# Token lists from products of ones-and-zeros rows, and a state scaled ahead of its addition

## The chip, the cores and the metric

The kernel runs on one core of a Trainium2 chip. A core has five engines with queues of their own, each strictly in order: TensorE (PE; its weight loads are shown apart as PEld), VectorE (DVE), ScalarE (ACT), GpSimd (POOL) and SyncE (SP), which here only issues transfers. Sixteen DMA engines move data; SP, ACT and POOL can all issue to them. The metric is the device time of one execution in microseconds (us).

## The reference, cut to what matters

Two layers on 4096 tokens (8 batches of 512) of 256 numbers.

```python
def L0_attn(u):        # a state-space layer, run forward and backward, chunks of 128 tokens
    ...
    states = einsum('bcln,bhcl,bclhp->bchpn', B, decay_states, x)
    new_states = einsum('bhzc,bchpn->bzhpn', decay_chunk, states)   # state * decay + addition
    ...
def L0_ffn(x):         # every token goes to its best of 8 experts (256 -> 1024 -> 256)
    p = softmax(x @ Wr + br); e = argmax(p)
    y = p[e] * (relu(x @ W1[e] + b1[e]) @ W2[e] + b2[e])
def L1_attn(x):        # attention, 16 heads, products of queries and keys over 512 tokens
    ...
def L1_ffn(x):         # two best of 8 experts, 512 places each; the last "expert" returns its input
    ...
```

The two expert layers matter here. In each, a program on the chip must turn "token t goes to expert e with weight m" into a list: which token stands at which place of an expert, and its weight. Layer 0 cuts the sorted tokens into 39 blocks of 128 rows (`NBLK`), each of one expert. Layer 1 has 7 experts with 512 places, 28 groups of 128 (`NSLOT1 // P`).

## The kernel before

**Start.** `rows_in` loads the tokens in four pairs of batches. For a pair DVE takes means and variances (L358), ACT normalises into `xn` (L366), PE transposes (L386), ACT copies the transposed tiles out (L387), PE makes the small projection with step sizes and the expert logits (L392), and ACT copies that into `proj` (L396). `xn` holds 272 numbers a row: 256 of the token, its number, its weight, and padding.

**Layer 0's lists.** `route0` makes the softmax, takes the best expert, ranks the tokens of each expert (`ranks`) and computes for each token the row `slot0` of a sorted copy `xd0` in DRAM. 32 indirect transfers from POOL (L473), 128 rows each, scatter the rows of `xn` to it. `xd0` has been filled with blank rows before (L376, number out of range), so that free rows are known. `step_sizes` works out step sizes and decays; `decays` and `edges` follow.

**The expert blocks of layer 0.** `blocks` is a generator: at each `yield` it has recorded one piece. `fetch` asks for the block's rows `xd` (SP, a plain load of 128 rows), and for `w1`, `b12` and `w2` (POOL, indirect by `w_idx`). A block is two halves of 16 PE instructions (L583) with bias and relu on ACT (L590) or DVE (L592), a turn of the next block's rows, and the second product (L604). The result is scaled by the weight that came with the row (`xd[:, DM+1]`) and scattered by the number that came with it to `yt0` (`put`, L559).

**The chunk loop.** 64 chunks (8 batches, 4 steps, 2 directions) are recorded by hand in one order for all engines (`manual_schedule`). For a chunk: `segments`, `cross`, `inside` (L1077), `before` (the old state's share: L1095 on PE, L1096 on DVE, L1097 on POOL), `pairs`, `behind` (the new state: L1103 on PE, the scaling L1109 on POOL, the addition L1112 on DVE). Between them `turn()` places parts of the next and last batch and `fill(1)` advances the generator chain `rows` (route0, then blocks) by a yield; when it has run out, each fill advances `late` instead. Ahead of the loop `send(k)` advances `rows` by k yields; it is used 39 times there in all, and those 39 yields are just route0's.

**The join of the layers.** `late` first loads the weights of the second layer (`second_weights`), then runs three chains in turn: `norm(b)` (read x1, add yt0 to it by a POOL transfer, normalise, write `xn1`), `turn(b)` (transpose, logits, and the projections of the attention), `route(lo, hi)` (ranks and places for a group of batches, for 0 to 4, 4 to 7 and 7 to 8). A batch is taken only when its chunks are done. `route` writes `slot1` and then scatters pairs of number and weight, 8 bytes a row, by 64 indirect transfers from POOL (L758) to `tab` in DRAM, which ACT's queue has cleared (L1256). What `late` has left at the end of the chunk loop is done between the first steps of layer 1's attention.

**Layer 1.** 128 steps of attention; `experts` loads the list `slots` from `tab`, gathers rows of `xn1` by it (L1297) and runs between the steps, paced by `due()`.

A tile of a pool with one buffer, asked for again under the same tag, must wait until all readers of the old one are done.

Of the kernel before, what the change touches and what calls it, by code (L numbers as in the profile page):

```python
# [40 lines left out]
DW = DM + 16  # L41
FAR = NSLOT1 * P
# [18 lines left out]
def tile_kernel(ctx: ExitStack, tc: tile.TileContext, t, out: bass.AP):  # L61
# [36 lines left out]
    blank = ctile("blank", [P, DW])  # L98
    G.memset(blank, 0.0)
    G.iota(blank[:, DM : DM + 1].bitcast(I32), pattern=[[0, 1]], base=NT, channel_multiplier=1)  # L100


    xd0 = dram.tile([NBLK * P, DW], FP, name="xd0", tag="xd0")
    yt0 = dram.tile([NT, DM], FP, name="yt0", tag="yt0")
    tab = dram.tile([NSLOT1, 2], FP, name="tab", tag="tab")
# [13 lines left out]
    def clear(dst, rows, lo, hi):  # L119

        n = rows // P
        A.dma_start(
            out=dst[: n * P, :].rearrange("(p r) d -> p r d", p=P)[:, lo:hi, :],
            in_=bc(blank[:, : dst.shape[1]], 1, [P, hi - lo, dst.shape[1]]),
        )

# [44 lines left out]
    def ranks(pool, bank, mask, hold):  # L171
# [18 lines left out]
        rank = pool.tile(shape, FP, name="rk_r", tag="rk_r")  # L190
        V.tensor_tensor(rank, cum, total, ALU.subtract)
        V.tensor_tensor(rank, rank, pre, ALU.add)
# [4 lines left out]
    def slots_of(pool, oh, where, tag):  # L197

        n = oh.shape[1]
        pick = pool.tile([P, n, NE], FP, name="so_p", tag="so_p")  # L200
        V.tensor_tensor(pick, oh, where, ALU.mult)
        s = pool.tile([P, n], FP, name="so_s" + tag, tag="so_s" + tag)
        V.tensor_reduce(s, pick, AX.X, ALU.add)
        return s

# [58 lines left out]
    def rows_qk():  # L264
# [8 lines left out]
    xs = ctx.enter_context(ExitStack())  # L273
    xn = xs.enter_context(tc.tile_pool(name="x0", bufs=1, side="right")).tile(
        [P, NTILE, DW], FP, name="xn0", tag="xn0"
    )
    G.memset(xn[:, :, DM:], 0.0)
    G.iota(xn[:, :, DM].bitcast(I32), pattern=[[P, NTILE]], base=0, channel_multiplier=1)
# [29 lines left out]
    w_in = ctile("w_in", [P, KC, 2 * P * HC + NXBC * P - DI], pool=l0c)  # L308
# [25 lines left out]
    slot0 = l0c.tile([P, NTILE], I32, name="slot0", tag="slot0")  # L334
# [15 lines left out]
    def rows_in():  # L350

        G2 = 2 * TPB
        for u, b0 in zip(us, order[::2]):
# [10 lines left out]
            V.scalar_tensor_tensor(nm, mv[:, :, 0], -1.0, rs, ALU.mult, ALU.mult)  # L364
            for i in range(G2):
                A.activation(  # L366
                    xn[:, b0 * TPB + i, :DM], u[:, i, :], AF.Identity,
                    bias=nm[:, i : i + 1], scale=rs[:, i : i + 1],
                )
            if b0 == order[0]:  # L370
                Y.dma_start(out=w_in, in_=t["w_in"])
            if b0 == order[2]:
                n = NBLK // B + 1
                for k in range(B):
                    lo, hi = k * n, min(NBLK, (k + 1) * n)
                    Y.dma_start(  # L376
                        out=xd0.rearrange("(p r) d -> p r d", p=P)[:, lo:hi, :],
                        in_=bc(blank, 1, [P, hi - lo, DW]),
                    )
            xTs = {}  # L380
            for b in both:
                xTs[b] = m2.tile([P, KC, S], FP, name="xT", tag="xT")
                for k in range(KC):
                    tp = bank("tp", [P, S], 0)
                    for c in range(TPB):
                        T.transpose(tp[:, c * P : (c + 1) * P], xn[:, b * TPB + c, k * P : (k + 1) * P], ident)  # L386
                    A.copy(xTs[b][:, k, :], tp)  # L387
            for b in both:
# [7 lines left out]
                A.copy(proj[:, b * TPB : (b + 1) * TPB, :], pp)  # L396
                if b > 1:
                    Y.dma_start(out=xtd[b], in_=xTs[b])
        return xTs

    def step_sizes():
# [6 lines left out]
        ea = big.tile([P, 2 * NH], FP, name="ea", tag="ea")  # L408
# [1381 lines left out]
```

## Time and profile before

Three runs took 2043.42, 2045.7 and 2048.68 us; the median is 2045.7.

| | |
|---|---|
| the profiled execution's own time | 2045.05 us |
| its span, first to last instruction | 2043.4 us |
| mean granted PE clock | 0.941 |
| PE busy | 1807.3 us (88%) |
| DVE busy | 1416.6 us (69%) |
| ACT busy | 1180.8 us (58%) |
| POOL busy | 683.8 us (33%) |
| data moved by DMA | 244.56 MB |
| L473, scatters of layer 0's rows | 32, 32.7 us of POOL |
| L758, scatters of layer 1's pairs | 64, 64.7 us of POOL |
| L1109, scaling of the state | 32, 35.5 us of POOL |
| DVE at L1112 waiting for L1109 | 68.2 us, 16 times, longest 11.6 |
| SP's queue at L533 (`xd` loads) waiting for scatters of L559 | 336.1 us, 31 times |

The stages in time: tokens in until 67.6 us; route0 and step sizes until 98.6; the first batch's parts until 153.3, where the first product of the chunk loop (L1077) runs; expert blocks beside the chunks until about 860; the join until the first experts of layer 1 at about 1260; attention and experts to the end. Times in the profile are from the span's start. A bracket at the end of a line of the timeline gives the idle time of that engine ahead of the instruction and what ended it.

### The profile page before, as it was taken

What the parts mean: (1) busy time and instruction counts of PE and PEld (TensorE: products, weight loads), DVE (VectorE), ACT (ScalarE), POOL (GpSimd) and SP (SyncE); (2) the same over time, 40 slices, a digit from 0 to 9 for tenths busy, and PEclk for the clock granted to TensorE, in tenths of its full rate; (3) what the DMA queues carried; (4) which work ended last, traced back from release to release, by engine and by line L of the source; (5) the groups of instructions that cost most, each with busy time, mean ns of one, the idle gap of its engine ahead of it and who ended that gap; (6) DMA issues with size and microseconds to landing.
All of it is one profiled execution on the core that took longest, in us unless ns stands there. A gap on an engine that the chain in (4) does not pass through costs nothing.

```text
span 2043.4 us, 33598 instructions
## 1 busy us (share of the span) xinstructions
PE 1807.3 (88%) x11768; PEld 1226.2 (60%) x11768; DVE 1416.6 (69%) x3296; ACT 1180.8 (58%) x2592; POOL 683.8 (33%) x620
## 2 busy tenths in 40 slices
PE   6458799999999999969878778999999999999997
PEld 5326577776776666635545545666666666666654
DVE  4574575766757585566672658888787878788885
ACT  4233354544544444345443237878788877788886
POOL 0265465654656555342247222111111111111030
PEclk9778899999999999979988768999999999999999
DMA  8035754555555455254532323131313131314171
GB/s 284 25 107 206 148 187 163 184 174 174 195 179 188 141 188 173 80 134 123 155 99 91 96 70 111 45 102 47 101 48 102 39 103 39 101 42 118 37 140 47
DMA packets 145895, 244.56 MB, mean 120 GB/s; under 512 B 26269, under 2 KB 106015, under 8 KB 133824
## 3 DMA queue, kind: packets, MB, share of 16 engines
q1 hardware_dynamic: 108080, 126.56, 20.1%
q0 software_dynamic: 33392, 115.18, 19.1%
q10 hardware_dynamic: 4256, 0.69, 0.4%
q8 instruction: 94, 1.54, 0.3%
q14 instruction: 73, 0.60, 0.1%
HBM read 183.93 MB, written 59.36 MB: 119 GB/s over the span
## 4 chain that ended last, share of the span: by engine, by line
PE 60%; DVE 12%; ACT 12%; issue 5%; DMA 4%; POOL 3%; SPq 0%; POOLq 0%; ACTq 0%; DVEq 0%
PE p_ps L1505 7%; PE y_ps L604 6%; PE pj L852 6%; PE h_ps L583 6%; ACT s L1498 6%; PE o_ps L1514 5%; PE e_hp L1333 4%; PE s_ps L1483 4%; PE e_yp L1346 4%; ACT pT L1506 3%; PE op L996 2%; PE seg L1039 2%; PE yd L1077 2%; PE sp L1103 2%; DVE cv L865 1%
## 5 line engine op out<-in xcount | busy, mean ns | idle before, releaser
L1488 DVE TENSOR_SCALAR s<-s_ps 128x512 f32<-128x512 f32 x512 | 318.1, 684 | 140.3 <-PE s_ps L1483 138.8
L1498 ACT ACTIVATE s<-s,ng 128x512 f32<-128x512 f32 x512 | 330.9, 717 | 23.2 <-DMA kT<-kd 23.2
L1490 DVE CUSTOM_DVE_ANT_0 s<-s,band 128x512 f32<-128x512 f32 x512 | 323.1, 687 | 0.0
L1506 ACT COPY pT<-p_ps 128x512 f32<-128x512 f32 x512 | 275.5, 588 | 61.2 <-PE p_ps L1505 54.3
L1505 PE MATMUL p_ps<-ident,s 128*128 128x128 f32 x2048 | 284.9, 282 | 21.8 <-ACT pT L1506 16.8
L1505 PEld LDWEIGHTS p_ps<-ident,s 128*128 128x128 f32 x2048 | 235.2, 143 | 95.7 <-ACT pT L1506 33.5
L1353 POOL DMA_INDIRECT x<-e_yo,slots x28 | 45.8, 1635 | 622.3 <-ACT e_yo L1352 622.3
L852 PE MATMUL pj<-xT,w_in 128*128 128x512 f32 x384 | 199.4, 645 | 18.0 <-DVE cv L865 10.1
L583 PEld LDWEIGHTS h_ps<-xdT,w 128*128 128x128 f32 x1248 | 151.1, 194 | 24.5 <-issue 23.5
L1483 PE MATMUL s_ps<-kT,qT 16*128 16x512 f32 x1024 | 159.4, 662 | 5.6 <-DMA kT<-kd 4.4
L583 PE MATMUL h_ps<-xdT,w 128*128 128x128 f32 x1248 | 154.8, 278 | 3.5 <-DMA w<-in_w_dram,w_idx 3.5
L865 DVE SCALAR_TENSOR_TENSOR cv<-pj,w_conv_w,cv 128x511 f32<-128x511 f32 (+2 forms) x192 | 143.2, 746 | 12.5 <-ACT cv L861 8.0
L604 PE MATMUL y_ps<-w,hT 128*128 128x256 f32 x624 | 151.1, 386 | 0.0
L1097 POOL TENSOR_TENSOR yT<-yT,ex 128x512 f32<-128x512 f32 (+1 forms) x48 | 59.3, 1235 | 243.7 <-DVE ex L1096 174.9
L604 PEld LDWEIGHTS y_ps<-w,hT 128*128 128x128 f32 x624 | 118.2, 194 | 34.9 <-issue 18.7
L1333 PE MATMUL e_hp<-e_xdT,e_w 128*128 128x256 f32 x448 | 121.6, 394 | 10.1 <-ACT e_hT L1336 9.1
L852 PEld LDWEIGHTS pj<-xT,w_in 128*128 128x128 f32 x384 | 70.2, 201 | 98.7 <-issue 81.7
L1514 PE MATMUL o_ps<-pT,vt 128*32 128x256 f32 x2048 | 127.5, 388 | 0.0
L1077 PE MATMUL yd<-mt,xdt 128*64 128x128 f32 x1024 | 77.1, 297 | 42.6 <-DVE mt L1071 23.4
L1346 PE MATMUL e_yp<-e_w,e_hT 128*128 128x256 f32 x448 | 113.3, 385 | 0.2 <-ACT e_hT L1336 0.2
L1514 PEld LDWEIGHTS o_ps<-pT,vt 128*32 128x32 f32 x2048 | 61.3, 111 | 84.4 <-issue 51.5
L1052 ACT ACTIVATE mt<-seg,mid 64x64 f32<-64x64 f32 x512 | 109.4, 309 | 0.8
(301 smaller groups left out, 3056.9 us busy)
## 6 DMA issues: line engine op xcount, KB each, us to landing
ex<-exd SPq DMA_DIRECT2D x96, 128.0 KB
fr<-fdd SPq DMA_DIRECT2D x64, 128.0 KB
od<-os SPq DMA_DIRECT2D x28, 256.0 KB
e_w<-in_ei_dram SPq DMA_DIRECT2D x7, 1024.0 KB
e_w<-in_eo_dram SPq DMA_DIRECT2D x7, 1024.0 KB
xd<-xd SPq DMA_DIRECT2D x39, 136.0 KB
xd<-blank SPq DMA_DIRECT2D x7, 680.0 KB
vd<-vt SPq DMA_DIRECT2D x16, 288.0 KB
```

The lines of the kernel that those rows point to most:

```text
L583: T.matmul(hp[:, i, :], w1[:, k * FF + f * P : k * FF + (f + 1) * P], xdT[:, k * P : (k + 1) * P], start=(k == 0), stop=(k == KC - 1),)
L604: T.matmul(yp, hT[f // 4][:, f % 4, :], w2[:, f * DM : (f + 1) * DM], start=(f == 0), stop=(f == FC - 1))
L852: T.matmul(pj, w_in[:, k, o * P : (o + 1) * P], self.xT[:, k, :], start=(k == 0), stop=(k == KC - 1))
L1333: T.matmul(hp, w1[:, k, f * P : (f + 1) * P], xdT[:, k, :], start=(k == 0), stop=(k == KC - 1))
L1346: T.matmul(yp, hT[:, f, c * P : (c + 1) * P], w2[:, f, :], start=(f == 0), stop=(f == FC - 1))
L1483: T.matmul(sp[i], self.q[r, cols], self.k[r, :], start=True, stop=True)
L1488: V.tensor_scalar(self.p[i], sp[i], -CLAMP, CLAMP, ALU.max, ALU.min)
L1490: V.tensor_tensor_reduce(out=self.p[i], in0=self.p[i], in1=band[:, at : at + S], scale=1.0, scalar=-3.0e38, op0=ALU.mult, op1=ALU.max, acc ...
L1498: A.activation(self.p[i], self.p[i], AF.Exp, bias=self.ng[:, i : i + 1])
L1505: T.transpose(pp[:, k, :], self.p[i][:, k * P : (k + 1) * P], ident)
L1506: A.copy(pT[i][:, :, cc * P : (cc + 1) * P], pp)
L1514: T.matmul(op[32 * i : 32 * i + 32, half * 2 * P : (half + 1) * 2 * P], self.v[:, k, h * (AD + 1) : h * (AD + 1) + 32], pT[i][:, k, :], st ...
```

## The change

Layer 0: `xn`, its numbers and padding are gone. ACT normalises in place, SP writes the rows to `xn0` in DRAM (8 stores), and the transposes read the same tiles. `proj` and one of two transposed tiles of the first two batches are copied by DVE, the former one pair later. `xd0` and its clears are gone. `route0` splits each place into block and row (`locate`), and `enter` builds, for eight tiles at a time, rows of ones and zeros on DVE and multiplies them on PE, adding up a table of number and weight for each place. `numbers` turns it into integers (a free place gives a number past the last token). The blocks gather their rows by it. `b12` becomes part of `w2`'s rows. `route0` has 8 yields in place of 39; ahead of the loop `rows` is advanced 9 times and then once with each of some 13 slots.

Layer 1: the same in place of `slot1`, `tab` and 64 scatters, two tiles at a time, one group of four entries for each batch and yield; the table stays in SBUF. `route` takes batches 0 to 5 and 5 to 8. `second_weights` yields three times more, `norm` twice more behind its first addition, `w_o` is loaded at the start of layer 1.

The chunk loop: the state's scaling on POOL stands in `before`, ahead of L1097, and not in `behind`. The first product of `start` is POOL's for the first batch. The clear of `tab` is gone, that of `xn1`'s last rows has another form.

```diff
+    def locate(pool, at):
+        n = at.shape[1]
+        i = pool.tile([P, n], I32, name="lc_i", tag="lc_i")
+        V.tensor_copy(i, at)
+        V.tensor_scalar(i, i, 7, None, ALU.logical_shift_right)
+        hi = pool.tile([P, n], FP, name="lc_h", tag="lc_h", bufs=2)
+        V.tensor_copy(hi, i)
+        lo = pool.tile([P, n], FP, name="lc_l", tag="lc_l", bufs=2)
+        V.scalar_tensor_tensor(lo, hi, -float(P), at, ALU.mult, ALU.add)
+        return lo, hi
+
+    def enter(pool, to, lo, hi, pair, first, last):
+        n, blocks = lo.shape[1], to.shape[1]
+        row_of = pool.tile([P, n, P], FP, name="en_r", tag="en_r")
+        V.tensor_tensor(row_of, bc(lo, 2, [P, n, P]), bc(iota_p, 1, [P, n, P]), ALU.is_equal)
+        of = pool.tile([P, n, blocks], FP, name="en_b", tag="en_b")
+        V.tensor_tensor(of, bc(hi, 2, [P, n, blocks]), bc(iota_p[:, :blocks], 1, [P, n, blocks]), ALU.is_equal)
+        what = pool.tile([P, n, blocks, 2], FP, name="en_w", tag="en_w")
+        V.tensor_tensor(what, bc(of, 3, [P, n, blocks, 2]), bc(pair, 2, [P, n, blocks, 2]), ALU.mult)
+        for i in range(n):
+            T.matmul(
+                to.rearrange("p b k -> p (b k)"), row_of[:, i, :], what[:, i].rearrange("p b k -> p (b k)"),
+                start=(first and i == 0), stop=(last and i == n - 1),
+            )
+
+    def numbers(pool, table, to):
+        none = pool.tile([P, table.shape[1]], FP, name="nu_n", tag="nu_n")
+        V.tensor_scalar(none, table[:, :, 0], 0.0, nowhere, ALU.is_equal, ALU.mult)
+        V.scalar_tensor_tensor(to, table[:, :, 0], -1.0, none, ALU.add, ALU.add)
...
-                A.copy(proj[:, b * TPB : (b + 1) * TPB, :], pp)
+                pps.append((b, pp))
...
+        tp = bank("tab", [P, NBLK, 2], "e")
+        n = 2 * TPB
+        for i in range(0, NTILE, n):
+            at = slice(i, i + n)
+            enter(big, tp, lo[:, at], hi[:, at], pair0[:, at, :], i == 0, i + n == NTILE)
+        V.tensor_copy(table0, tp)
+        numbers(big, table0, number0)
...
-                        Y.dma_start(out=w, in_=xd0[j * P : (j + 1) * P, :])
+                        G.indirect_dma_start(
+                            out=w, out_offset=None, in_=xn0, bounds_check=NT + P - 1, oob_is_err=True,
+                            in_offset=bass.IndirectOffsetOnAxis(ap=number0[:, j : j + 1], axis=0),
+                        )
...
-                for i in range(lo * TPB, hi * TPB):
-                    for k in range(2):
-                        one = G.indirect_dma_start(
-                            out=tab, out_offset=bass.IndirectOffsetOnAxis(ap=slot1[:, i, k : k + 1], axis=0),
...
+                    for i in range(0, n, TPB):
+                        yield
+                        tp = late_bank("tab1", [P, NSLOT1 // P, 2])
+                        for h in range(0, TPB, 2):
+                            at = slice(i + h, i + h + 2)
+                            own = slice(lo * TPB + i + h, lo * TPB + i + h + 2)
+                            for k, (row_, block) in enumerate(where):
+                                enter(
+                                    pool, tp, row_[:, at], block[:, at], pairs[:, own, k, :],
+                                    h == 0 and k == 0, h == 2 and k == 1,
+                                )
+                        V.tensor_tensor(slots, slots, tp, ALU.add)
...
+                if not self.last:
+                    G.tensor_tensor(
+                        heads(st), heads(st), bc(dec_all[:, self.d, self.i, :], 2, HP), ALU.mult
+                    )
                 V.tensor_tensor(self.ex, self.ex, yo, ALU.mult)
                 G.tensor_tensor(self.yv, self.yv, self.ex[:, :, self.span], ALU.add)
...
-                    d = self.d
-                    G.tensor_tensor(
-                        heads(st), heads(st), bc(dec_all[:, d, self.i, :], 2, HP), ALU.mult
-                    )
                     V.tensor_tensor(st, st, sp, ALU.add)
```

## The prediction

> **What bounds the kernel now.** I read the busy tenths in 40 slices first, then busy time by stages, then the chain of waits and the timeline at the places where TensorE (PE) is not full.
>
> ```profile
> PE   6458799999999999969878778999999999999997
> DMA  8035754555555455254532323131313131314171
> 75.00:100.00 25.00, 2.48 (x7) 1.85 (x8) 22.55 (x51) 0.00 (x0) 10.68 (x10) 0.54 0.15 51
> 100.00:125.00 25.00, 18.22 (x40) 5.60 (x39) 12.61 (x21) 9.57 (x21) 14.71 (x15) 0.71 0.24 84
> 125.00:150.00 25.00, 14.02 (x35) 5.93 (x33) 21.97 (x28) 9.33 (x19) 15.75 (x15) 0.80 0.42 136
> 250.00:800.00 550.00, 535.24 (x3240) 387.69 (x3239) 369.97 (x631) 260.46 (x731) 315.65 (x273) 0.99 0.54 178
> 860.00:1260.00 400.00, 312.68 (x1563) 190.73 (x1562) 249.04 (x682) 175.86 (x407) 155.90 (x152) 0.82 0.38 110
> ```
>
> The columns of a stage are its limits, its length, then busy time and count of PE, weight loads, DVE, ACT, POOL, then granted clock, DMA share and GB/s. From 250 to 800 us PE is busy 97%: there only PE work counts, and work of other engines is free. Two stages have holes: the start (0 to 250) and the join of the layers (860 to 1260, PE idle 22%). The change works in both. From 1300 on PE is about 95% busy again and nothing is edited, so what the joints win or lose reaches the end.
>
> **The start, part by part.** Up to 67.6 us four pairs of batches run in lockstep, because ACT copies the projection out before it normalises the next pair:
>
> ```profile
> 35.04 0.24 ACT L396 COPY proj<-pp 128x96 f32<-128x96 f32 x1 [2.65 <-PE pp L392]
> 38.46 0.24 ACT L396 COPY proj<-pp 128x96 f32<-128x96 f32 x1 [3.18 <-PE pp L392]
> 31.56 6.86 PE L392 MATMUL pp<-w_w_small,xT 128*128 128x24 f32 x32
> ```
>
> A pair takes 13.4 us (norms begin at 11.88, 25.24, 38.59). With the copy on DVE, ACT normalises under those products; what is left on PE is 6.9 us of products and about 4.2 us of transposes, 11.1. Three pairs save 3 x 2.3 and the last pair's wait for a transposed tile (2.3 us, on the store of xT) shrinks with three buffers: 8 us. Low end 0, should 4 MB of new row stores take the place of the 5.3 MB of clears that are gone; high end 9.
>
> The lists of layer 0 replace 32 scatters, which sat on POOL (about 1.0 us and 0.30 issue each, 86 to 137 us) beside DVE work, so removing them wins nothing there. They add, on the DVE path between slot0 (84.98 us) and the step sizes (85.07): five small operations for row and block, 1.0; four groups of eight tiles. In a group DVE compares 1024 numbers a row (1.23, as L1071 at its best), 312 (0.48, between 0.43 for 256 and 0.69 for 512) and multiplies 624 (0.84): 2.55. Then PE makes 8 products, each two instructions: L392 has the same weights and a short moving side, 6.86/32 = 0.214 us, so 3.4; the later L583 runs 16 in 1.95. The row tile has one buffer, so the next group's compare waits for these products and the two add up, with 0.2 for the hand-overs. 4 x (2.55 + 3.4 + 0.2) = 24.6. Then copy and numbers 0.8, and the block's weight index, which moves ahead of the step sizes, 2.1 (98.73 to 100.98 now). Sum 28.5 late; 22.7 with the fast products. I take 28.5, since PE is as idle there as at L392.
>
> The trace grants PE 0.54 of its clock in 75 to 100 us. The Trainium skill (TensorE: Matmul & The Clock Gate, Part 1: The HAM clock gate) says the clock halves after an idle window of some 3.4 us and is given back after one that is busy. By it four groups with 2.55 us of DVE between them could even keep the clock full, 22.7 by the sum above; the slow row speaks for 28.5.
>
> In exchange 14 pieces of the expert blocks of layer 0, 2.4 blocks, are dealt out ahead of the chunk loop. A block is 8.1 us of PE (4 x 1.95 first halves and products of L604 at 1.89 per 8, and 0.4 transposes). In the loop that is PE time saved: 2.4 x 8.1 = 19.4. Ahead of the loop the pieces lie in a stretch (98.6 to 153.3 us) with 17.8 us of PE idle between 100 and 150; they need 18.6 us at the fast rows and about 30 at the slow ones (16 of L583 took 3.75 at 161 us), and DVE and ACT must wait for them in order. I add 4; ends -3 (PE's clock rises) and +12. The first x by fr product goes to POOL for the first batch: DVE is spared 4 x 0.69, but its neighbours slow down:
>
> ```profile
> 143.85 2.98 DVE L922 SCALAR_TENSOR_TENSOR yT<-x,w_d_rep,yT 128x511 f32<-128x511 f32 x2
> 258.32 1.53 DVE L922 SCALAR_TENSOR_TENSOR yT<-x,w_d_rep,yT 128x511 f32<-128x511 f32 x2
> ```
>
> The first ran beside POOL's products of L938, the second did not. So POOL gives back what DVE wins: 0. The Trainium skill (SBUF — State Buffer, Who interferes with whom) has the rule: a DVE instruction with two inputs in SBUF contends with a GpSimd instruction that reads SBUF, and one blocks fully. It speaks against moving work to POOL; the pair above agrees, 2.98 against 1.53.
>
> Two stalls go. The first expert weights are asked for early and not at 155 us, where the chain of waits has 5.75 us of DMA w<-in_w_dram,w_idx: -5.75 (0 if the gathers come late too). And this one:
>
> ```profile
> 212.04 0.58 ACTq L1256 DMA_DIRECT2D tab<-blank  x1
> 210.00:220.00 10.00, 10.00 (x80) 7.39 (x79) 7.74 (x17) 5.70 (x18) 7.67 (x7) 1.00 0.60 21
> 220.00:230.00 10.00, 10.00 (x54) 6.04 (x53) 2.88 (x4) 2.64 (x4) 6.23 (x7) 1.00 0.90 56
> 244.69 0.69 DVE L915 TENSOR_TENSOR yT<-x,fr 128x512 f32<-128x512 f32 x1 [12.35 <-DMA fr<-fdd]
> ```
>
> The clear of tab goes out in pieces of 8 bytes; the DMA engines are 60 and 90% busy and move 21 and 56 GB/s. A store of 16 KB (fdd) issued at 221.56 is 19.24 us on the chain of waits, and PE idles 11.0 us between 230 and 250. The clear is gone: -11 (low -5, should other transfers hold the store).
>
> Start: -8 + 28.5 + 4 - 19.4 - 5.75 - 11 = **-11.7 us**.
>
> The block fetches: 39 loads of xd leave SP's queue, where they waited 336 us for scatters, and come to POOL as gathers; 39 fetches of b12 leave POOL. A gather is 1.14 (L1297) and a b12 fetch 1.15, so POOL is even. SP's queue is freed, but PE is full beside it: 0.
>
> **The join.** Three more yields after the second weights' loads: PE waited 7.5 us for w_dn: -7.5 (0 to -7.5). Two more after the first read-add: DVE waited 7.3 us for xr<-yt and PE 9.85 behind it: -7 (0 to -9.9). Then POOL:
>
> ```profile
> 1076.21 0.69 DVE L1112 TENSOR_TENSOR st<-st,sp 128x512 f32<-128x512 f32 x1 [5.69 <-POOL st L1109]
> 1093.23 0.69 DVE L1112 TENSOR_TENSOR st<-st,sp 128x512 f32<-128x512 f32 x1 [11.64 <-POOL st L1109]
> 1110.41 0.69 DVE L1112 TENSOR_TENSOR st<-st,sp 128x512 f32<-128x512 f32 x1 [7.62 <-POOL st L1109]
> ```
>
> Chunks come every 17.1 us because POOL holds eight scatters of 1.28 between its products, and the state's scaling stands behind them. The first 32 of the 64 scatters lie here. DVE waits 25 us, PE idles 8.6 in 1060 to 1120: I take -12 between (ends -5 and -20). Scaling ahead of the addition, elsewhere in the join: 5 us of L1112 waits left, -3 (0 to -5). POOL's addition to yT then waits one product of 1.1 us longer; nothing waits for it soon. One pass of route fewer spares some 45 DVE instructions of 0.2: -6 (0 to -9).
>
> Against it stand 8 groups of 4 entries. An entry is 0.92 us of DVE (0.43 for 256 numbers, 0.21 for 56, 0.28 for 112) and 4 PE instructions of 0.117; again one buffer, so DVE and PE take turns. PE loses three turns of 0.92 + 0.15 and 1.9 of its own: 5.1 a group, 41 for eight, less the 22% that PE idles there anyway: +33. Ends: 15 (PE's own work alone) and 56 (turns on both engines, 7.0 a group). Join: -7.5 - 7 - 12 - 3 - 6 + 33 = **-2.5 us**.
>
> Together -14.2. The profiled execution took 2045.05 us (span 2043.4 and 1.65 around it), 0.65 under the median of 2045.7; so **2031 us**, own range 2005 to 2039.
>
> **Rivals.**
> 1. *The turns of the lists decide* (slower). Each small product waits for DVE and each compare for PE; the join has DVE and PE handing over already (PE's waits for DVE add up to over 50 us in 800 to 1260). Entries at 56 (+23) and the start's pieces at +12 (+8): 2031 + 31 = 2062. It decides from 5.9 us a group, where 8 groups eat the -14.2. Against it: DVE runs ahead of PE where PE is full.
> 2. *The early blocks buy idle fills* (no change). Late work is gated by finished batches, so blocks that end earlier may leave empty turns in 860 to 1150 and not time. 14.4 of the 19.4 are lost: 2045.
> 3. *POOL was the whole trouble of the join.* Without scatters the entries hide (+15 for +33) and -20 for -12, -9.9 for -7: 2031 - 29 = 2002.
>
> That it does not do what it says is unlikely: every scatter line is deleted.
>
> **Numbers.** Forecast 0.52, rival 1 0.28, rival 2 0.10, rival 3 0.10. Under 0.3% (6 us) this kernel's measurement can't tell from no change. Faster: nine tenths of the forecast, all of rival 3 and a little of rival 2, 0.60; same 0.12; slower 0.28. Range 1994 to 2068.
>
> **What would show it.** Right: the last projection copy at 58 to 62 us; da at 112 to 119 us (98.6 now); the first yd product at 168 to 180 (153.3) with two blocks done; no PE hole near 240; L1112 waits under 35 us in all (68.2); a list group in the join of 5 us on PE. Wrong: groups of 6 us or more, waits of h_ps for the gathered xd, or a PE idle share in the join that does not fall below 22%.

## The result, and the profile after

Four runs of the kernel after took 2073.52, 2060.61, 2068.46 and 2061.94 us, median 2065.2; the kernel before, beside it, 2044.56. The ratio is 1.0103, 95% interval [1.0063, 1.0143]: 1% slower, where 2031 us was forecast. The profiled execution is the slowest of the four, 2073.52 us (span 2071.8), 28.5 more than that of before (2045.05); the medians differ by 20.6.

The busy tenths of the kernel after, in 40 slices of 51.8 us; the third line is the granted clock in tenths:

```profile
PE   6567999999999999789877867999999999999997
PEclk7589999999999999899967766999999999999999
DMA  7044554554645462445302312131313131314161
```

The same stages as before, then the two places that matter. Columns as in the prediction: limits, length, busy time and count of PE, PEld, DVE, ACT and POOL, granted clock, DMA share, GB/s:

```profile
75.00:100.00 25.00, 14.77 (x64) 13.95 (x64) 9.56 (x13) 0.00 (x0) 0.00 (x0) 0.50 0.00 1
100.00:125.00 25.00, 9.96 (x31) 5.06 (x32) 19.32 (x32) 4.97 (x14) 10.09 (x9) 0.61 0.54 201
125.00:150.00 25.00, 20.09 (x90) 11.77 (x88) 13.85 (x23) 9.43 (x19) 4.64 (x5) 0.93 0.24 84
250.00:800.00 550.00, 535.26 (x3256) 387.08 (x3255) 373.68 (x626) 262.84 (x737) 310.54 (x270) 0.99 0.52 174
860.00:1260.00 400.00, 317.26 (x1522) 197.55 (x1524) 246.15 (x647) 156.05 (x368) 81.34 (x73) 0.80 0.31 92
1040.00:1100.00 60.00, 42.79 (x158) 29.86 (x159) 28.03 (x96) 5.53 (x15) 4.49 (x4) 0.59 0.07 22
1230.00:1270.00 40.00, 19.78 (x94) 13.52 (x92) 23.84 (x84) 4.92 (x9) 0.12 (x1) 0.54 0.02 7
```

PE's fifth slice (207 to 259 us) stands at 9 for 7 before: the hole near 240 is gone (230 to 250 us: 20.00 of 20 busy), and POOL's work in the join is halved (81 for 156 us). But in 1040 to 1100 and 1230 to 1270 no engine is full, PE's clock falls to 0.59 and 0.54, and ACT, POOL and the DMA engines all but stop. Those are the list groups of layer 1: five in the first routing pass, three in the second. The timeline of the kernel after inside one group, DVE and PE:

```profile
1048.72 0.42 DVE L217 TENSOR_TENSOR en_r<-lc_l,iota_p 128x256 f32<-128x256 f32 x1 [3.98 <-PE tab L223]
1049.06 0.21 DVE L219 TENSOR_TENSOR en_b<-lc_h,iota_p 128x56 f32<-128x56 f32 x1
1049.31 0.28 DVE L221 TENSOR_TENSOR en_w<-en_b,pairs 128x112 f32<-128x112 f32 x1
1049.64 1.10 PE L223 MATMUL tab<-en_w,en_r 128*128 128x56 f32 x4 [0.95 <-DVE en_w L221]
1050.78 0.42 DVE L217 TENSOR_TENSOR en_r<-lc_l,iota_p 128x256 f32<-128x256 f32 x1 [1.20 <-PE tab L223]
...
1051.69 1.10 PE L223 MATMUL tab<-en_w,en_r 128*128 128x56 f32 x4 [0.95 <-DVE en_w L221]
...
1053.75 1.10 PE L223 MATMUL tab<-en_w,en_r 128*128 128x56 f32 x4 [0.95 <-DVE en_w L221]
```

An entry comes every 2.05 us: PE works 1.10 and waits 0.95 for DVE, DVE waits 1.20 for PE. Four such entries are 8.2 us, and all that is queued behind them on both engines waits too. Over the eight groups, PE is busy 32.8 us with the 128 instructions and waits 37.0 us for their rows, 69.8 together (busy time, mean ns of one, then the waits and what ended them):

```profile
L223 PE MATMUL tab<-en_w,en_r 128*128 128x56 f32 x128 | 32.8, 406 | 37.5 <-DVE en_w L221 37.0 <-ACT lat L246 0.5
```

The lines of the start that answer to those of before, from the timeline of the kernel after: the last projection copies, on DVE now, a pair of the first batch's scaled additions (L960), the first `yd`, and the second batch's first product with `fr`:

```profile
52.90 0.26 DVE L383 COPY proj<-pp 128x96 f32<-128x96 f32 x1 [2.55 <-PE pp L420]
56.31 0.26 DVE L383 COPY proj<-pp 128x96 f32<-128x96 f32 x1 [3.16 <-PE pp L420]
...
157.28 1.79 DVE L960 SCALAR_TENSOR_TENSOR yT<-x,w_d_rep,yT 128x511 f32<-128x511 f32 x2
...
178.69 1.98 PE L1115 MATMUL yd<-mt,xdt 128*64 128x128 f32 x16 [7.45 <-DVE mt L1109]
...
252.04 0.68 DVE L953 TENSOR_TENSOR yT<-x,fr 128x512 f32<-128x512 f32 x1
```

The tokens are in at 56.31 us for 67.6, DVE no longer waits 12.35 us for `fr`, and the scaled additions of the first batch took 1.79 a pair at most, where the slow pair before took 2.98; the first `yd` is 25.4 us later, inside the recorded 168 to 180.

Where the 28.5 us come from, by the starts of `yd` products (chunks counted from 0) and of layer 1's score products (`s_ps`) in the two profiled executions:

| place | before | after | after − before |
|---|---|---|---|
| chunk 0 | 153.30 | 178.69 | +25.4 |
| chunk 16 | 403.86 | 409.22 | +5.4 |
| chunk 40 | 763.08 | 769.36 | +6.3 |
| chunk 57 | 1053.00 | 1027.28 | −25.7 |
| chunk 59 | 1078.09 | 1106.60 | +28.5 |
| chunk 63 | 1138.90 | 1144.54 | +5.6 |
| first score step | 1175.27 | 1173.91 | −1.4 |
| seventh score step | 1240.83 | 1274.64 | +33.8 |
| own time | 2045.05 | 2073.52 | +28.5 |

The kernel after was 26 us ahead at chunk 57. The first pass's groups cost it 54 us in two chunks. Part of that comes back, as before pays there for its scatters (chunks of 17.1 us), and the second pass's groups take 35 again. These are two single executions: two more of after had the first `yd` at 174.65 and 178.90 and chunk 40 at 764.42 and 770.31.

### The profile page after: what moved, and what is told of

Same layout as the page of the kernel before. It is cut to its first block, busy times and chain, and to the rows that moved or that the text cites. A ratio compares the mean times of both kernels' runs of the same rounds, so it can differ in the third digit from the quotient of the medians.

```text
span 2071.8 us, 33710 instructions
## 1 busy us (share of the span) xinstructions
PE 1839.1 (89%) x11956; PEld 1256.2 (61%) x11956; DVE 1461.9 (71%) x3374; ACT 1178.4 (57%) x2581; POOL 585.2 (28%) x528
## 3 DMA queue, kind: packets, MB, share of 16 engines
q10 hardware_dynamic: 1040, 0.66, 0.1%
## 4 chain that ended last, share of the span: by engine, by line
PE 39%; ACT 11%; DVE 9%; issue 1%; DMA 1%; SPq 0%; ACTq 0%; DVEq 0%; POOLq 0%
PE p_ps L1540 8%; ACT s L1533 6%; PE o_ps L1549 5%; PE e_hp L1368 4%; PE s_ps L1518 4%; PE e_yp L1381 4%; ACT pT L1541 3%; PE tab L223 2%; PE op L1034 2%; DVE s L1525 1%; PE pj L889 1%; DVE s L1523 1%; PE qp L258 1%; PE yd L1115 1%; PE fin L1481 1%
## 5 line engine op out<-in xcount | busy, mean ns | idle before, releaser
L1388 POOL DMA_INDIRECT x<-e_yo,number x28 | 45.7, 1633 | 629.1 <-ACT e_yo L1387 622.9
L889 PE MATMUL pj<-xT,w_w_in 128*128 128x512 f32 x384 | 197.1, 638 | 6.2 <-DVE z L995 4.0
L637 PEld LDWEIGHTS y_ps<-w,hT 128*128 128x128 f32 x624 | 118.3, 195 | 34.9 <-issue 17.1
L1368 PE MATMUL e_hp<-e_xdT,e_w 128*128 128x256 f32 x448 | 121.5, 394 | 11.2 <-ACT e_hT L1371 9.1
L889 PEld LDWEIGHTS pj<-xT,w_w_in 128*128 128x128 f32 x384 | 70.1, 200 | 85.3 <-issue 73.5
L1061 POOL TENSOR_TENSOR au<-da,half 128x512 f32<-128x512 f32 x64 | 77.7, 1215 | 149.4 <-PE seg L1077 145.3
L1124 DVE TENSOR_TENSOR yT<-yT,yd 128x512 f32<-128x512 f32 (+1 forms) x64 | 43.8, 685 | 102.1 <-PE yd L1115 97.3
```

The costliest lines, as they stand in the source:

```text
L637: T.matmul(yp, hT[f // 4][:, f % 4, :], w2[:, f * DM : (f + 1) * DM], start=(f == 0), stop=(f == FC - 1))
L889: T.matmul(pj, w_in[:, k, o * P : (o + 1) * P], self.xT[:, k, :], start=(k == 0), stop=(k == KC - 1))
L1368: T.matmul(hp, w1[:, k, f * P : (f + 1) * P], xdT[:, k, :], start=(k == 0), stop=(k == KC - 1))
```

## The experiments

The terms of the recorded sum have letters here. At the start: A the loading of tokens (−8), B the lists of layer 0 (+28.5), C the early pieces of the blocks (+4), D what those pieces save in the loop (−19.4), E the expert weights asked for early (−5.75), F the clear of `tab` gone (−11). In the join: G the yields behind the weights' loads (−7.5), H those behind the read-add (−7), I the scatters gone (−12), the scaling (−3), the pass of `route` spared (−6), J the list groups of layer 1 (+33).

The kernel before ran beside every set of kernels, and its medians moved from set to set (2044.6, 2055.4, 2045.4, 2060.9, 2047.3, 2059.5 us); kernels that ran in several sets moved less (after: 2065.2, 2068.0, 2070.6; without entries: 1994.6, 1996.0). So what one edit is worth is read in us between changed kernels, and the ratios to the kernel before stand beside it. The two columns on the right are from the traces: from chunk 57 to chunk 63 (first pass), and from the fifth to the seventh score step (second pass).

| kernel | us | ratio to before | 57 to 63 | steps 5 to 7 |
|---|---|---|---|---|
| before | | | 85.9 | 11.9 |
| after | 2065.2 | 1.0103 [1.0063, 1.0143] | 117.3 | 47.2 |
| after_again | 2068.0 | 1.0125 [1.0089, 1.0161] | | |
| after_third | 2070.6 | 1.0046 [1.0024, 1.0069] | | |
| no_entries | 1994.6 | 0.9691 [0.9656, 0.9726] | 71.9 | 12.5 |
| no_entries_again | 1996.0 | 0.9744 [0.9717, 0.9771] | 68.3 | 12.7 |
| only_compares | 2017.8 | 0.9859 [0.9839, 0.9879] | 81.5 | 18.6 |
| only_products | 2015.2 | 0.9838 [0.9817, 0.9859] | 78.8 | 25.2 |
| buffers | 2038.4 | 0.9917 [0.9887, 0.9947] | 95.6 | 36.4 |
| spread | 2059.9 | 1.0053 [1.0026, 1.0079] | 107.8 | 36.5 |
| late_add | 2037.9 | 0.9884 [0.985, 0.9917] | 97.8 | 30.9 |
| pipelined | 2036.7 | 0.9876 [0.986, 0.9893] | 92.7 | 30.6 |
| scatters | 2038.3 | 0.9901 [0.9863, 0.9938] | 82.6 | |
| old_scaling | 2086.5 | 1.0134 [1.0095, 1.0173] | | |
| old_scaling_again | 2084.5 | 1.0118 [1.0096, 1.014] | | |
| old_yields | 2089.6 | 1.0157 [1.011, 1.0204] | | |
| late_blocks | 2065.1 | 1.0109 [1.0074, 1.0144] | | |
| start_buffers | 2059.5 | 1.007 [1.0042, 1.0098] | | |
| buffers_both | 2035.0 | 0.9873 [0.9855, 0.9892] | | |
| best | 2028.9 | 0.9908 [0.9887, 0.9929] | 95.7 | 30.6 |

### What the list groups cost: no entries

```diff
-                        tp = late_bank("tab1", [P, NSLOT1 // P, 2])
-                        for h in range(0, TPB, 2):
...
-                        V.tensor_tensor(slots, slots, tp, ALU.add)
...
             G.memset(slots, 0.0)
+            G.iota(
+                slots[:, :, 0], pattern=[[P, NSLOT1 // P]], base=1, channel_multiplier=1,
+                allow_small_or_imprecise_dtypes=True,
+            )
```

> Leaves out the list groups of layer 1 (compares, products and the addition to slots), with the yields kept; the token numbers are filled with a fixed count instead, so that the gathers and scatters behind stay as many and as large, though the rows of layer 1's experts and their weights are not the reference's. It prices the whole term J. Theory (the turns of the groups decide): the traces show a swing of some 54 us at chunks 57 to 59 and some 28 us at the start of layer 1, so 60 to 80 us come off the 2065 us of the kernel after: 1985 to 2005. As recorded in the prediction (term J is +33): 2032. Rival (something else in the join costs the time: state scaling, the yields, the gathers): 2050 or more.

1994.6 us: the groups cost 71 us, about 9 each, and not 33 (by the ratios, 62 to 89). This agrees with the 69.8 us that PE is busy with them or waits for their rows in the profile. By the recorded sum the rest of the change gains 47 us (−14.2 − 33); against the kernel before beside it this kernel gains 61, and 51 where it ran again. So without these groups the change is a gain, and they alone turn it into a loss.

### One buffer: turns

```diff
-        row_of = pool.tile([P, n, P], FP, name="en_r", tag="en_r")
+        size = n * (P + 3 * blocks)
+        if lo_rows:
+            whole = row("en")[:, :size]
+        else:
+            whole = pool.tile([P, size], FP, name="en", tag="en", bufs=bufs)
+        a, c = n * P, n * (P + blocks)
+        row_of = whole[:, :a].rearrange("p (n q) -> p n q", n=n)
...
-                                    h == 0 and k == 0, h == 2 and k == 1,
+                                    h == 0 and k == 0, h == 2 and k == 1, lo == 0, 3,
```

> Only the storage of a list entry of layer 1 changes: a row tile out of the pool of eight for the first five groups, one of three buffers for the last three, where there was one buffer. The instructions are the same. Theory (one buffer makes DVE and PE take turns): DVE runs ahead, a group takes 0.92 + 4 x 1.1 = 5.3 us or less instead of 8.2, 8 x 2.9 = 23 us come off: about 2042. Rival (the products on a slow PE are the cost, whatever DVE does): 4 x 1.1 of 8.2 stays anyhow and the rest is covered elsewhere, 2058 or more. PE's waits for en_w, 0.95 a turn, must be gone in the trace either way.

2038.4 us: 27 us come off, 4 more than the theory's 23, and the kernel is faster than the kernels before and after. In its timeline the sixteen PE instructions of a group stand in one piece:

```profile
1050.28 2.98 PE L229 MATMUL tab<-en 128*128 128x56 f32 x16 [0.68 <-DVE en L227]
1059.06 2.87 PE L229 MATMUL tab<-en 128*128 128x56 f32 x16 [1.39 <-DVE en L227]
1073.83 3.63 PE L229 MATMUL tab<-en 128*128 128x56 f32 x16 [0.85 <-DVE en L227]
```

They take 2.9 to 3.7 us, with at most one wait for DVE, at their head. Over the eight groups:

```profile
L229 PE MATMUL tab<-en 128*128 128x56 f32 x128 | 26.1, 371 | 18.6 <-DVE en L227 17.7
```

The waits fell by 19.3 us and the work by 6.7, as PE was slow for less of it; together that is the 27. Still, 43 us stay above the kernel without entries, and 26.1 + 17.7 make about these.

### What the other 43 us are: pieces, addition, pipeline

`spread` cuts a group into two halves, each a piece of filling work of its own:

```diff
+                        for h in range(0, TPB, 2):
+                            tp = late_bank("tab1", [P, NSLOT1 // P, 2])
...
+                                    k == 0, k == 1, lo == 0, 3,
...
+                            V.tensor_tensor(slots, slots, tp, ALU.add)
+                            yield
```

> The kernel with the row tiles as buffers (0.9917 of before), and besides every group of layer 1 cut in two halves of two entries, each a piece of filling work of its own with its own bank and its own addition to slots. The kernel without entries stood at 0.9691, so 46 us of the lists are left. Theory (what is left comes from four entries recorded back to back, DVE 3.7 us in one piece): half of them or more hide between the chunks' own work, 0.980 or less. Rival (the 3.7 us of DVE and 3 to 4 us of products of a group lie on the path of the join wherever they are put): 0.988 to 0.996, no better than with the buffers alone, and the additions cost 0.2 us a group.

Wrong on both sides: 2059.9 us, 21 slower than the buffers alone, though its ten runs range from 2045 to 2069. The timeline of DVE in `spread` shows where it waits:

```profile
1080.33 0.21 DVE L801 TENSOR_TENSOR slots<-slots,tab 128x56 f32<-128x56 f32 x1 [5.91 <-PE tab L229]
1096.35 0.69 DVE L1157 TENSOR_TENSOR st<-st,sp 128x512 f32<-128x512 f32 x1 [4.00 <-PE sp L1152]
```

Each half ends in an addition that waits for PE, up to 5.91 us, with the chunk's own DVE work behind it. The sixteen additions wait 24.2 us in all, where the eight of `buffers` wait 10.6. So `late_add` records the addition one piece later, here `made` being DVE's compares and `entered` PE's products:

```diff
+                        new = made(i, TPB)
+                        if held is not None:
+                            add(held)
+                        held = entered(new)
```

And `pipelined` also makes the rows one piece ahead, in pieces of two entries:

```diff
+                        new = made(i, 2)
+                        if held is not None:
+                            add(held)
+                        held = entered(ready) if ready else None
+                        ready = new
```

> The kernel with the row tiles as buffers, and the addition of a group's bank to slots is recorded one piece later, behind the compares of the next group; the last three groups of layer 1 (the second pass) share one bank and one addition. Where the group was cut in two (spread), DVE stood 16.8 us in ten additions for PE's products, each with the chunk's own work queued behind, and the time rose to 1.0053. Theory (each piece pays for every time that DVE waits for PE's products in order): the additions no longer wait and two round trips of the second pass are gone, 10 to 20 us under the buffers alone (0.9917): 0.982 to 0.987. Rival (DVE's own 3.7 us and PE's 3 us a group are what is left): 0.989 to 0.995.

> As late_add, but in pieces of two entries, and each piece makes the rows of the next one on DVE, the products of the present one on PE and the addition of the one before: no engine waits for another within a piece. Theory (the turns are the cost, not the instructions): down towards the kernel without entries (0.9691), 0.972 to 0.982. Rival (instructions on the path): as late_add, or worse, as there are ten pieces for five, 0.99.

2037.9 and 2036.7 us: next to nothing below the buffers. In both the second pass got shorter (31 for 36 us), where three banks and additions became one; the first changed by +2 and −3. That is the rival's side. `pipelined` has ten pieces in the first pass as `spread` has, and is 23 us faster: that speaks for the waits as the cost of `spread` and not for the smaller pieces, though the rows made ahead and the one bank of the second pass differ too. So the instructions were taken apart, beside a floor (the kernel without entries, run again) that has neither. `only_compares`:

```diff
-        for i in range(n):
+        for i in range(n if to is not None else 0):
...
-                        tp = late_bank("tab1", [P, NSLOT1 // P, 2])
+                        tp = None
```

`only_products`:

```diff
+                        for h in range(2 * TPB):
+                            T.matmul(
+                                tp.rearrange("p b k -> p (b k)"), still[:, h % 2 * P : h % 2 * P + P],
+                                still[:, 2 * P + h % 2 * 56 : 2 * P + h % 2 * 56 + 56],
+                                start=h == 0, stop=h == 2 * TPB - 1,
+                            )
                         V.tensor_tensor(slots, slots, tp, ALU.add)
```

> The kernel without the list groups of layer 1, as before (their compares, products and additions to slots are left out, fixed token numbers instead), on the same chip as the two kernels below, as their floor. Every theory: 0.966 to 0.973.

> The kernel with row tiles as buffers, but of the list groups of layer 1 only DVE's compares and multiplications are left; the products and the additions to slots are left out (fixed token numbers instead). 8 x 3.7 = 30 us of DVE. Theory I (in the join the engines hand over in order, so each instruction's time lies on the path whichever engine has it): 24 to 30 us over the floor, 0.981 to 0.985. Theory II (only the meeting of DVE and PE costs): within 10 us of the floor, 0.969 to 0.974.

> Of the list groups of layer 1 only the products, from a tile that never changes, and the additions to slots are left; DVE's compares and multiplications are left out (fixed token numbers instead). 8 groups of 16 PE instructions, 2.9 us warm to 4.4 us on the slow clock, and a wait of DVE for the bank. Theory I (each instruction's time lies on the path): 20 to 32 us over the floor, 0.979 to 0.985. Theory II (only the meeting costs): within 10 us of the floor, 0.969 to 0.974. If compares and products together exceed the 46 us that buffers left, they overlap in part there.

21.8 us over the floor for the compares, 19.3 for the products; together 41, near the 43 that the buffers left. That is theory I, with sizes just under its lower ends (24 and 20), and not theory II (10 at most). The 19.3 hold more than PE's own time: the additions to `slots` are still there, and DVE waits 13.8 us at them for the products, which no run takes apart. Two of the groups of `only_products`, whose operands are always ready:

```profile
1055.86 1.89 PE L788 MATMUL tab<-still 128*128 128x56 f32 x16
1060.48 1.89 PE L788 MATMUL tab<-still 128*128 128x56 f32 x16
```

0.118 us an instruction: the fast price of the prediction holds where PE does not wait. Seven groups took 1.89 to 1.99 us; the eighth, behind a wait of 6.72 us, took 3.66. By these differences the 71 us of the groups are 22 of compares, 19 of products with their additions, and some 30 of turns (exchanges in which each engine waits for the other), with the slow clock that goes with them.

### Scatters again

```diff
-                        where.append(locate(pool, at))
...
+                        one = G.indirect_dma_start(
+                            out=tab, out_offset=bass.IndirectOffsetOnAxis(ap=slot1[:, i, k : k + 1], axis=0),
...
-            both.append(itertools.chain.from_iterable(route(*g) for g in ((0, 5), (5, 8))))
+            both.append(itertools.chain.from_iterable(route(*g) for g in ((0, 4), (4, 7), (7, 8))))
...
+                    A.dma_start(out=tab.rearrange("(p r) d -> p r d", p=P), in_=blank)
```

> Undoes the lists of layer 1: scattered pairs as in the kernel before, in its three passes, with the table cleared in one dense store instead of pieces of 8 bytes; everything else (lists of layer 0, early blocks, yields, scaling ahead) stays as after. Theory (the groups of the join are the loss): the terms of the prediction without J, I and the spared pass are -14.2 - 33 + 12 + 6 = -29, so about 2016. Rival (another part of the change costs the time): 2050 or more.

2038.3 us, 22 above the theory: 43 us above the kernel without entries, where the prediction gave scatters and the spared pass 12 + 6. The scatters were dear too; the lists, as written, are dearer by 27. And `buffers` took 2038.4 us beside it: the lists of layer 1 with buffers are no better than the scatters that they replace, so the gain of the faster versions over the kernel before comes from the rest of the change.

### The start

> The kernel after, but the 14 early pieces of the expert blocks are not dealt out ahead of the chunk loop (the first weights are still fetched early). By the recorded terms C and D the pieces cost 4 us at the start and save 19.4 later: 15 us slower than after, a ratio near 1.018. Rival 2 of the prediction (blocks that end earlier only leave empty turns): within 5 us of after, 1.008 to 1.013. The first yd product should come some 4 to 10 us sooner than 178.7 us.

```diff
             def both(work=None):
                 slot(work)
-                send(1)
```

2065.1 against 2068.0 us of after beside it (`after_again`), where 15 us more were expected. The first `yd` comes 4.3 us sooner (170.38 for 174.65, or 8.3 and 8.5 sooner than in the other two profiles of after), so term C was 4 or somewhat more; the 19.4 of term D are not there. In the stage that term D counted on, both kernels do the same. First `late_blocks`, then `after_again`:

```profile
250.00:800.00 550.00, 535.72 (x3256) 387.09 (x3255) 371.44 (x635) 262.93 (x737) 314.88 (x276) 0.99 0.53 180
```

```profile
250.00:800.00 550.00, 535.28 (x3231) 386.79 (x3230) 372.77 (x632) 260.93 (x731) 306.94 (x267) 0.99 0.50 170
```

As the loop is written, it takes a fixed number of pieces a chunk, whichever they are. From chunk 40 to 63 `late_blocks` needs 375.8 us and `after_again` 372.1: the early pieces bring back 3.7 at most, and the first profile of after needs 375.2, so even these can't be told from the spread.

> The kernel after, unchanged, beside the other kernels of this call on the same chip. Every theory: a ratio of 1.006 to 1.014 to the kernel before, as measured first.

> The kernel after, but the lists of layer 0 are entered in eight groups of four tiles with two buffers, in the same memory, where there were four groups of eight tiles and one buffer. Theory (turns, as in the join): DVE 8 x 1.5 = 12 us and PE 3.7 x 4 = 14.7 us overlap, so the lists take 16 to 17 us instead of 25, and the first yd product and the end come 8 us sooner: 0.4% under after. Rival (a late start is made up anyway in the loop's empty turns, as the lag shrank from 25 us at the first chunk to 6.7 at the seventh): within 3 us of after.

```diff
-        n = 2 * TPB
+        n = TPB
...
-            enter(big, tp, lo[:, at], hi[:, at], pair0[:, at, :], i == 0, i + n == NTILE)
+            enter(big, tp, lo[:, at], hi[:, at], pair0[:, at, :], i == 0, i + n == NTILE, bufs=2)
```

2059.5 us, 8.5 under after beside it, the theory's 8, though the intervals of the two ratios overlap. The products of all eight groups stand in one piece from 76.27 to 90.52 us. The first `yd` stands at 169.32 us. Of that lead over `after_again` (5.3 us) 0.6 is left at chunk 63; of the 9.4 and 9.6 over the other two profiles of after, 8.7 and 6.3 are left. Those two speak against the rival, and so do the kernels with both edits below, which keep their lead of 9 to 11 us to chunk 63.

### The join's other terms

```diff
                         add(b)
                         yield
-                        yield
-                        yield
...
             yield
-            yield
-            yield
-            yield
             A.activation(band, band, AF.Abs)
```

> The kernel after without the three yields behind the second weights' loads and without the two behind the read-add (terms G and H, -7.5 and -7): by the prediction 14.5 us (0 to 17) slower than after, a ratio near 1.019. In the traces after gained 14 us on before between chunks 40 and 48, which says the same. Rival (the wait is only moved, as the filling work is a fixed amount): within 4 us of after, 1.009 to 1.014.

2089.6 us, 19 to 24 above after by us; by the ratios 0.3 to 1.1%, or 7 to 23 us. The direction is the recorded one, and 14.5 us lies inside the ratios' span and under the us.

```diff
-                if not self.last:
-                    G.tensor_tensor(
-                        heads(st), heads(st), bc(dec_all[:, self.d, self.i, :], 2, HP), ALU.mult
-                    )
...
+                    d = self.d
+                    G.tensor_tensor(
+                        heads(st), heads(st), bc(dec_all[:, d, self.i, :], 2, HP), ALU.mult
+                    )
                     V.tensor_tensor(st, st, sp, ALU.add)
```

> Undoes only the move of the state's scaling ahead of the addition. Theory: the move is worth 3 us (0 to 5), so 2065 to 2070. Rival (POOL scaling earlier delays its additions to yT, or slows DVE beside it, and this is the loss): 2045 to 2055.

> The kernel after, unchanged, as the partner of the next kernel on one chip. If a kernel's us agree between calls and only the kernel before moves: 2062 to 2070 us. If the chips' states move all kernels together: its ratio stays at 1.010 to 1.0125 whatever the us.

> The kernel after with the state's scaling behind the yoff products undone, beside the kernel after on one chip. As recorded (3 us, 0 to 5): 2065 to 2071. By the us of the first run of it: 2080 to 2088, 20 us over the kernel after, in which case the term was seven times too small.

Side by side 2070.6 us for after, 1.0046 [1.0024, 1.0069], and 2084.5 with the scaling undone, 1.0118 [1.0096, 1.014]: the move is worth 14 us, not 3. What DVE's addition to the state waits for, over the whole run, first with the scaling undone, then in after (columns: sum, times, longest):

```profile
DVE st L1150 <- POOL st L1147: 45.7, 17, 7.2
DVE st L1150 <- PE sp L1141: 17.4, 5, 4.9
```

```profile
DVE st L1150 <- PE sp L1145: 38.2, 16, 4.9
```

So DVE waits 38.2 us there for 63.1: part of the wait for POOL only became a wait for PE. Some 8 of the 14 us lie where PE is full: from chunk 0 to 40 the two profiles with the scaling undone need 598.9 and 598.1 us, the three of after 589.8 to 591.4.

### Faster versions

`buffers_both` joins the edits of `buffers` and `start_buffers`, `best` those of `pipelined` and `start_buffers`.

> Buffers for the entries of both layers: row tiles in layer 1, and eight groups of four tiles with two buffers in layer 0. Alone they stood at 0.9917 and, against 1.0125 of after on one chip, 1.0070. Theory (the two places add up): 0.986 to 0.988. Rival (the start's gain is taken up by the loop): 0.990 to 0.993.

> The pipeline of layer 1's lists (pieces of two entries, rows made one piece ahead, the addition one piece later) together with the lists of layer 0 in eight groups of four tiles and two buffers. Alone: 0.9876, and 0.5% of after for the start. Theory (the parts add up): 0.981 to 0.986. Rival (the loop takes up the start's gain): 0.987 to 0.990.

2035.0 us, 0.9873 [0.9855, 0.9892], and 2028.9, 0.9908 [0.9887, 0.9929]: both are faster than the kernels before and after, and in us the start's buffers gain 3 to 8 more. `buffers_both` lies where its theory had it. The ratio of `best` is above both of its expectations, its us below all others with full lists; the kernel before stood at 2047.3 beside it and at 2060.9 beside `buffers_both`, so which of the two is better is told by the us alone.

## Why the prediction was wrong

**The step that failed is term J:** "PE loses three turns of 0.92 + 0.15 and 1.9 of its own: 5.1 a group, 41 for eight, less the 22% that PE idles there anyway: +33". The turn was right (0.95 seen). Two things were not. PE's own part was priced at the fast row of 0.117 us, and the turns themselves keep PE slow: 1.10 us for four instructions, 0.275 each, so 8.2 a group and 66 for eight. And the discount for idle time was not there: the 66 us, taken out, gave back 71. PE idles in the join because it waits in order, and what is put between two hand-overs lengthens the wait; 17.3 us of products whose operands were ready moved the end by 19 (with the additions and their waits), and compares that take DVE 25 to 30 us by 22. At the start the same prediction had taken the slow row, 0.214, because PE idled there.

**Rival 1 named the mechanism** and its threshold (decides from 5.9 us a group, real 8.2), at 2062 us. Its own size was too small (+23 over the forecast for the entries; the groups were +38), so that it comes so near the 2065 measured is in part luck.

**Term by term.** A: last projection copy at 56.31 us, 11.3 sooner, for 8 (58 to 62 was the mark). B: four groups in 25 us for 24.6, `da` at 115.2, inside the 112 to 119. C: 4.3 to 8.5 for 4. D: 0 to 3.7 for 19.4, the second wrong step; rival 2, given a chance of 0.10, had it (early blocks leave empty turns and not time). That late work is paced and gated is read from the code; no run shows it singly. E and F: no hole near 240; A, B, C, E and F alone make +7.75. Chunk 40 stands at +6.3, +1.3 and +7.2 in the three profiles of after, and the 8 us that the scaling gains by then are in that, so the five are some 2 to 8 us dearer than recorded; of them only C was undone singly. G and H: some 20 for 14.5 by us. Scaling: 14 for 3; only the 25 + 5 us of waits in the join were counted, and the rest of its 68.2 over the run was called free, as PE is full there, where 8 of the 14 us turned up. I and the pass: 43 for 18. The waits of L1150 for POOL are gone altogether (under 35 was the mark), those for PE are 38.2 for 18.9 before. PE's idle share of the join is 20.7%, below the 22%, yet PE was busier with slow products, so the mark said nothing.

With these sizes the recorded sum of −14.2 becomes about 0 (J +38, D +17, I and pass −25, scaling −11, G and H −5). Measured is +20.6, +22.6 and +11.2. The edits are not independent, and the kernel before moves by as much from set to set; that remainder stays open. Taken together, all terms but J came out nearly as recorded: 2045.05 − 47.2 = 1998 us, and the kernel without the groups took 1994.6 and 1996.0. So J's 38 us are about the whole miss of 34; that the other errors, D and the scatters above all, cancel is luck. How much of the turns is the slow clock and how much the waiting was not taken apart beyond the 6.7 and 19.3 us of `buffers`. Whether the compares would hide on another engine was not tried.

## What to carry to other kernels

Where two engines hand over in order and neither is full, idle time is little cover: count a new instruction there at nearly its whole time (here on DVE and on PE), and count a producer and consumer that share one buffer as the sum of both. Look for the free buffer first (here the chunks' own row tiles), before changing what is computed. A piece of filling work that ends in a wait for another engine can cost that wait once per piece, so cutting it smaller can make it worse. And price what is to be replaced as carefully as its replacement: scatters and buffered lists came out the same.

## What the runs showed of the hardware

PE's clock did not come back under small products with full weight loads. In `start_buffers` PE made 64 instructions of 128x78 (32 products) without a break, 0.223 us each, and its granted clock stayed at half:

```profile
80.00:84.00 4.00, 4.00 (x19) 3.96 (x20) 3.29 (x7) 0.00 (x0) 0.00 (x0) 0.50 0.00 0
84.00:88.00 4.00, 4.00 (x21) 3.96 (x20) 3.26 (x9) 0.00 (x0) 0.00 (x0) 0.50 0.00 0
```

In the join, waits of 0.95 us between 1.10 us of products went with 0.50 (`after_third`, 1080 to 1100 us), while products of the same size among the chunks' own work ran at 1.00 in `only_products` (1060 to 1080 us), 0.118 us each for 0.275. In the first group of `after_third` PE turned slow, from 0.65 to 1.10 us for four instructions:

```profile
1045.06 0.63 PE L223 MATMUL tab<-en_w,en_r 128*128 128x56 f32 x4 [0.49 <-ACT lat L246]
1046.65 0.65 PE L223 MATMUL tab<-en_w,en_r 128*128 128x56 f32 x4 [0.95 <-DVE en_w L221]
1048.25 1.10 PE L223 MATMUL tab<-en_w,en_r 128*128 128x56 f32 x4 [0.95 <-DVE en_w L221]
```

In the 10 us ahead of that PE had no gap above 0.95 us. The Trainium skill (TensorE: Matmul & The Clock Gate, Part 1: The HAM clock gate) has the full clock after one busy window of some 3.4 us; the 14.25 us above do not show that. Its section on HAM oscillation asks for no idle gap above some 3.4 us; here gaps of 0.95 were enough beside such products. What the clock counts can't be told from these runs.
